# Statistics taken at each update of the residual, slot rows transposed two slots ahead, and bias rows and range test moved: a four-layer gated decoder on one core

## The chip, the cores and the metric

The kernel runs on one core of one Trainium2 chip. The metric is the device time of one execution in microseconds (us). The time before is the median of three runs; the profile is of a further execution. Engines are named as in the profile: PE (TensorE matmul), PEld (its weight loads), DVE (VectorE), ACT (ScalarE), POOL (GpSimd) and SP (SyncE, here a DMA queue).

## What is computed

x is [16, 128, 256] in float32: 16 sequences (b) of 128 rows with 256 features. Eight updates follow each other, each with the layer norm of x as input and a gate tanh(g) as factor:

```
x = x + tanh(g_xattn[0]) * xattn0(ctx, ln(x), ...)      # 16 heads of 16
x = x + tanh(g_ffn[0])   * moe0(ln(x))                  # 8 experts, best 2, hidden 1024, gelu
x = x + tanh(g_xattn[1]) * xattn1(ln(x), ctx, ...)      # softmax over the queries, biases
x = x + tanh(g_ffn[1])   * (ln(x) @ base + b + lora by softmax gates)
x = x + tanh(g_xattn[2]) * xattn2(ctx, ctx, ln(x), mask)
x = x + tanh(g_ffn[2])   * (moe2(ln(x)) + shared expert) # 8 experts, best 2, hidden 512, swiglu
x = x + tanh(g_xattn[3]) * xattn3(ctx, ln(x))           # keys: ctx and x together, 8 heads of 64
x = x + tanh(g_ffn[3])   * moe3(ln(x))                  # 8 experts, best 2, hidden 256, silu

def ln(x): (x - mean) / sqrt(var + 1e-5)
```

## The kernel before

x stays on the chip as 16 tiles `xs[b]` of [128 rows, 256]. They are worked in 4 blocks (`blk`) of 4. A norm of a block (`ln_block`, or `residual` in layer 3) is a chain over three engines: `ln_stats` takes bn_stats and bn_aggr of the four tiles on DVE (lines 242, 243), `inverse_sd` takes Ln and Exp on ACT and a Newton step on DVE (lines 219 to 232), `normalized` makes xn on ACT (257, 261), PE transposes it (284) and ACT copies it back (288).

Attention (`attend`) has its order on PE, ACT and DVE written by hand: everything between runs in program order on these engines. Steps over b make scores, values and output; the output's last operation adds into xs[b] (`add_scaled`, line 320). Between their parts they call `tick()`, which advances each waiting job (a generator) whose count has run out; a job's `yield n` asks for n ticks. Jobs are the preparation of the next block (with `fetch`, which adds an expert layer's output to xs, line 509), and what lies `behind` a block: in layers 0, 2 and 3 `Moe.front`, in layer 1 `Lora.run`. In the last stretch of `attend` (`late`) every yield counts as one tick.

An expert layer sorts its rows. `front` takes the norm, the router's logits (366), softmax and best two, works out a place for each row and scatters the rows to DRAM (`xg`, line 473, eight indirect DMAs on POOL for each block); `plan` says which expert each of 39 slots of 128 rows belongs to. Then slots run: SP loads rows (`xr`, line 689) five slots ahead and weights by expert; PE transposes the rows (722), DVE copies them (`xT`, 724); PE does the two matmul layers (1349, 1525 or 1573, and 759); DVE weighs the output (`y`, 765 or 767); POOL scatters it to DRAM (`yd`, 768) by row numbers `to` (745), which have OUT = 8 buffers. Slots that are surely full start early, beside the attention's last block (layer 0), or beside the last front (layer 3). Of an iteration in `slots` the order is:

```python
first(s + near)
hT = yield from hidden(get, lane(s), xTs.pop(s), lambda *ps: when(s, *ps))
turn(s + 1)
hidden_of.append((s, hT))
if len(hidden_of) > depth:
    finish(*hidden_of.pop(0))
weigh(s + 1)
load(s + far)
second(s + near2)
```

Slots outside `attend` and other operations that stand outside it in the program are ordered by a planner, by its own costs and by what they depend on; it may put them between the operations of `attend`. Two such are of use here. `split_biases` (line 2001 on) makes of four bias rows three bfloat16 parts each, which PE adds by one matmul; three of the rows are read from `rows`, a tile loaded once at the start (line 2070). `Watch.fine` (1014 to 1019) compares sums of range with a bound; POOL collects them (1012). The result of that test decides at the end whether a slower general version runs.

Of the kernel before, what the change touches and what calls it, by code (L numbers as in the profile page):

```python
# [31 lines left out]
NE = 8  # L32
# [29 lines left out]
SURE = 2 * B + 1  # L62
OUT = 8
LANES = 3
# [26 lines left out]
def kernel(ctx: ExitStack, tc: tile.TileContext, a: dict, out: bass.AP):  # L91
# [142 lines left out]

    def ln_stats(srcs, twice=False):


        n = len(srcs)
        mv = stat.tile([P, n, 2], F32, tag="mv", name="mv", bufs=4)
        for i, src in enumerate(srcs):  # L240
            st = stat.tile([P, 6], F32, tag="bnst", name="bnst", bufs=4)
            nc.vector.bn_stats(st, src)
            nc.vector.bn_aggr(mv[:, i, :], st)
            if i % 2 and i < n - 1:
                yield 1
        rstd = yield from inverse_sd(mv[:, :, 1], n, twice)
        return mv, rstd

    def normalize(dst, src, mv, rstd, i):
# [18 lines left out]
    def block(blk):  # L268
        return range(blk * BPB, (blk + 1) * BPB)

    def ln_block(blk, see=None):


        mv, rstd = yield from ln_stats([xs[b] for b in block(blk)])
        if see is not None:
            see(rstd)
        xns = yield from normalized([xs[b] for b in block(blk)], mv, rstd)
        yield 4
        xt = xtpool.tile([P, KC, TB], F32, tag="xnT", name="xnT")
        for pair in range(BPB // 2):  # L280
            ps = ps_x.tile([P, KC, 2 * S], F32, tag="x", name="ps_ln")
            for j in range(2):
                for k in range(KC):
                    nc.tensor.transpose(
                        ps[:, k, j * S:(j + 1) * S],
                        xns[:, pair * 2 + j, k * P:(k + 1) * P], ident,
                    )
            nc.scalar.copy(xt[:, :, pair * 2 * S:(pair + 1) * 2 * S], ps)
            yield 1 if pair == 0 else 3
        return xns, xt  # L290
# [10 lines left out]

    def thirds(tag, bias_row, rest):

        t = rpool.tile([P, D], BF16, tag=tag, name="bias3", bufs=1)
        first, second, third = (slice(i * 32, (i + 1) * 32) for i in range(3))
        nc.vector.tensor_copy(t[0:96], bias_row[0:96])
        nc.vector.tensor_tensor(rest[0:96], bias_row[0:96], t[0:96], ALU.subtract)
        nc.vector.tensor_copy(t[second], rest[second])
        nc.vector.tensor_copy(t[third], rest[third])
        nc.vector.tensor_tensor(rest[third], rest[third], t[third], ALU.subtract)  # L310
        nc.vector.tensor_copy(t[third], rest[third])
        return t
# [19 lines left out]
    def softmax8(lg):  # L332
        m = tiny("sm_m")
        nc.vector.tensor_reduce(m, lg, AX.X, ALU.max)
        d = small("sm_d")
        nc.vector.tensor_tensor(d, lg, bc(m), ALU.subtract)
        e = small("sm_e")
        nc.scalar.activation(e, d, AF.Exp)
        yield 3
        s = tiny("sm_s")  # L340
        nc.vector.tensor_reduce(s, e, AX.X, ALU.add)
        r = tiny("sm_r")
        nc.vector.reciprocal(r, s)
        p = small("sm_p")
        nc.vector.tensor_tensor(p, e, bc(r), ALU.mult)
        return p
# [28 lines left out]
    class Moe:  # L375
# [4 lines left out]
        def __init__(self, layer, wg, turn, see=None):  # L380
            self.layer, self.wg, self.turn, self.see = layer, wg, turn, see
            self.carry = region
            self.done = None
            self.scatters, self.returns = [], []

# [3 lines left out]
        def front(self, blk, plan=None):  # L389

            xns, xnT = yield from ln_block(blk, self.see)
            lg = yield from router_logits(xnT, self.wg, NE)
            soft = softmax8(lg)
            next(soft)
            if self.layer == 2:
                yield 3
                p = finish(soft)
                key = small("key")
                nc.vector.tensor_tensor(
                    key, p, row("gate_b")[:, None, :].to_broadcast([P, BPB, NE]), ALU.add  # L400
                )
            else:
                key = lg
# [94 lines left out]
        def fetch(self, pool, blk):  # L498
# [8 lines left out]
            for i, b in enumerate(block(blk)):  # L507
                for j in range(2):
                    nc.vector.tensor_tensor(xs[b], xs[b], ys[i][:, j], ALU.add)
                yield 1  # L510

# [115 lines left out]
        def slots(self, n, plans, lanes, get, fetch1, fetch2, hidden, nf, far, depth):  # L627
# [126 lines left out]
            def finish(s, hT):  # L754
# [9 lines left out]
                if bias is None:  # L764
                    nc.vector.tensor_scalar(y, po, c[:, 1:2], None, ALU.mult)
                else:
                    nc.vector.scalar_tensor_tensor(y, po, c[:, 1:2], bias, ALU.mult, ALU.add)  # L767
                self.unordered(nc.gpsimd.indirect_dma_start(  # L768
# [14 lines left out]
            yield 1  # L783
            turn(0)
            weigh(0)
            hidden_of = []
            for s in range(n):
# [3 lines left out]
                hT = yield from hidden(get, lane(s), xTs.pop(s), lambda *ps: when(s, *ps))  # L791
                turn(s + 1)
                hidden_of.append((s, hT))
# [209 lines left out]
    class Watch:  # L1003
# [9 lines left out]

        def fine(self, good):

            eq = stat.tile([P, self.n], F32, tag="wz", name="wz", bufs=1)
            nc.vector.tensor_scalar(eq, self.sum, HUGE, None, ALU.is_le)
            nc.vector.tensor_reduce(good, eq, AX.X, ALU.add)
            return self.n * P
# [4 lines left out]
    class Fast16:  # L1024
# [184 lines left out]
        def output(self, b, tick):  # L1209
# [7 lines left out]
            if self.bias is not None:  # L1217
                add_row(py, self.bias)
            add_scaled(b, py, self.gate)
            tick()  # L1220

# [5 lines left out]
    def attend(parts, most=(99, 1), filler=None, open_end=False):  # L1227
# [29 lines left out]
        with tc.manual_schedule(engines=IN_ORDER):  # L1257

            tc.keep_in_program_order(nc.scalar.add_instruction(
                mybir.InstLoadActFuncSet(  # L1260
                    name=nc.get_next_instruction_name(), ins=[], outs=[], act_func_set_id=LN_EXP
                )
            ))
            ready = ahead(*blocks[0][:2], 0)
            for n in range(len(steps) + 2):
# [6 lines left out]
                if n < len(steps):  # L1272
                    if n % BPB == 0:

                        while any(job in jobs for job in ready):
                            tick()
                        if n // BPB + 1 < len(blocks):
                            att, before, _, blk = blocks[n // BPB + 1]
                            ready = ahead(att, before, blk)
                    att, b = steps[n]  # L1280
                    att.scores(b, tick)
# [81 lines left out]
    class Lora:  # L1363
# [10 lines left out]
        def run(self, blk):  # L1374
# [30 lines left out]
            for i, b in enumerate(block(blk)):  # L1405
# [7 lines left out]
                add_row(po, self.bias)  # L1413
                add_scaled(b, po, tgf(1))
                yield 1

# [194 lines left out]
    class Attention3:  # L1611
# [4 lines left out]
        def run(self, blk):  # L1616
# [3 lines left out]
            cts, ys = [], []  # L1620
            mv, rstd = finish(ln_stats([xs[b] for b in block(blk)]))
            for i, b in enumerate(block(blk)):
# [94 lines left out]
    class Fast3:  # L1717
# [106 lines left out]
        def residual(self, blk, before):  # L1824

            yield from before
            xb = [xs[b] for b in block(blk)]
            mv, both = yield from ln_stats(xb, twice=True)
            t = self.pool.tile([P, KC, TB], F32, tag="kvx", name="kvx")
# [124 lines left out]
        def output(self, b, tick):  # L1954
            oT = self.os.pop(b).rearrange("p i c s -> p (i c) s")
            py = ps_x.tile([P, D], F32, tag="x", name="ps_y")
            for k in range(4):
                nc.tensor.matmul(
                    py, lhsT=oT[:, k, :], rhs=self.w[3][:, k, :], start=(k == 0), stop=(k == 3)
                )  # L1960
            add_scaled(b, py, self.gate)
            tick()

# [35 lines left out]
    wgs, biases = {}, {}  # L1999

    def split_biases(t):

        nc.vector.tensor_scalar(row("l2_bo"), row("l2_bo"), 1 / DOWN, None, ALU.mult)
        for i, name in enumerate(("l1_bo", "l2_bo", "base_b")):
            biases[name] = thirds(name, row(name), t[:, 1 + i, 0:D])
        nc.vector.tensor_scalar(row("l2_bo"), row("l2_bo"), DOWN, None, ALU.mult)
        biases["sb"] = thirds("sb3", t[:, 0, 0:D], t[:, 1, 0:D])

    def layers(fast):
        first_turn = 1 if fast else 4  # L2010

# [34 lines left out]
        with tc.tile_pool(name="context", bufs=1) as cpool, ExitStack() as for_mid:  # L2046
# [16 lines left out]
            with tc.tile_pool(name="att0", bufs=2) as pool:  # L2063
# [16 lines left out]
                def clear(blk):  # L2080
                    if blk == 1:
# [9 lines left out]
                        for i in range(0, ROWS, n * P):  # L2091
# [5 lines left out]
                            )  # L2097
                    if blk == 2 and fast:
                        mask.extend(mask_by_keys(cpool, mi))
# [30 lines left out]
            with for_slots, tc.tile_pool(name="lanes0", bufs=2) as pool:  # L2130
                lanes = lanes + lane0(pool, LANES - len(lanes))
                job = slots0(moe, NSLOT - n, plans[-1:], lanes, tiles(fpool, bufs0))
                for i, _ in enumerate(job):
                    if i == 24:
                        ws = [attention_weights(layer, wpool) for layer in (1, 2)]
                        if not biases:

                            t = stat.tile([P, BPB, ROW], F32, tag="xn", name="bias_rows", bufs=3)
                            nc.sync.dma_start(
                                out=t[:, 0, 0:D],  # L2140
                                in_=a["l2_b2"][NE:NE + 1].to_broadcast([P, D]),
                            )
                    if i == 48 and not biases:
# [99 lines left out]
        with tc.tile_pool(name="last", bufs=1) as pool:  # L2243
            moe3.last(pool)

    layers(fast=True)

    watches = (watch, watch1, watch3)
    good = const.tile([P, len(watches)], F32, tag="good", name="good")
    want = sum(w.fine(good[:, i:i + 1]) for i, w in enumerate(watches))  # L2250
    ps = ps_x.tile([1, len(watches)], F32, tag="x", name="ps_good")
# [102 lines left out]
```

## Time and profile before

| | |
|---|---|
| runs | 1712.75 us median (1705.27, 1712.75, 1713.97) |
| profiled execution | 1708.5 us, of which the span is 1706.8 |
| PE busy | 1557.9 us (91%), granted clock 0.96 |
| PEld, DVE, ACT, POOL busy | 1197.2, 892.7, 636.6, 285.2 us |
| DMA | 169.29 MB, mean 99 GB/s |

Stages by the timeline: attention of layer 0 until about 150 us, its slots until 425, layers 1 and 2 (attention and Lora) until 840, layer 2's slots until 1237, attention of layer 3 until 1520, the last slots until 1673, the last additions until 1707. A row of the timeline has start, duration, engine, line, operation, out<-in, and in brackets the idle time before it with what ended it. A row of the waits has who waited for whom, the total in us, the number of times and the longest. "issue" is a wait for nothing that the profile shows.

### The profile page before, as it was taken

To read this page: it belongs to the slowest core of one execution; us is meant where nothing else is said; L and a number is where in the kernel's file an instruction comes from. 1 tells how busy PE (TensorE), PEld (TensorE's weight loads), DVE (VectorE), ACT (ScalarE), POOL (GpSimd) and SP (SyncE) were. 2 spreads that over 40 slices of the span, in tenths; PEclk is the share of its full clock that TensorE was granted. 3 is DMA by queue.
4 is the path that set the end of the run, shared out by engine and by line. 5 is a ranking of instruction groups with operands and counts; after the bars stand their busy time and mean duration, and the time that the engine had idled before them with its cause. 6 is when DMAs were issued, how large, how long until landed. Compare 5 with 4: busy or idle time off the path is not lost. (4 is left out here: it accounts for less than half of the span.)

```text
span 1706.8 us, 34879 instructions
## 1 busy us (share of the span) xinstructions
PE 1557.9 (91%) x12803; PEld 1197.2 (70%) x12803; DVE 892.7 (52%) x2915; ACT 636.6 (37%) x1504; POOL 285.2 (17%) x364
## 2 busy tenths in 40 slices
PE   4998999999889999998999999999989999986891
PEld 2666889999455566664459999999836665666891
DVE  2676521221477655665545555556724645556554
ACT  3554533345444454544224333334443323223010
POOL 4122411111000000221100111111100002114433
PEclk8998999999988999899999999999999999998996
DMA  9505675342200000110054323411220100033855
GB/s 336 216 27 181 202 254 166 116 144 86 87 26 1 1 14 14 39 39 26 26 192 149 132 70 98 153 30 30 94 68 26 38 2 26 20 113 109 271 161 184
DMA packets 110456, 169.29 MB, mean 99 GB/s; under 512 B 16697, under 2 KB 83710, under 8 KB 110272
## 3 DMA queue, kind: packets, MB, share of 16 engines
q1 hardware_dynamic: 92320, 118.28, 22.0%
q0 software_dynamic: 13392, 43.37, 6.8%
q10 hardware_dynamic: 4560, 5.25, 0.9%
q8 instruction: 108, 1.77, 0.4%
q14 instruction: 76, 0.62, 0.1%
HBM read 268.42 MB, written 48.18 MB: 185 GB/s over the span
## 5 line engine op out<-in xcount | busy, mean ns | idle before, releaser
L1525 PE MATMUL ps_w<-xT,w 128*128 128x128 f32 x2304 | 266.4, 275 | 0.0
L1525 PEld LDWEIGHTS ps_w<-xT,w 128*128 128x128 f32 x2304 | 264.0, 192 | 2.1
L768 POOL DMA_INDIRECT yd<-y,to x117 | 118.2, 1011 | 574.2 <-DVE y L767 382.7
L759 PE MATMUL ps_e<-w,hT 128*128 128x256 f32 x848 | 197.8, 380 | 3.0 <-DVE hT L1430 1.3
L759 PEld LDWEIGHTS ps_e<-w,hT 128*128 128x128 f32 x848 | 154.6, 190 | 22.8 <-PE ps_w L678 2.2
L1533 ACT ACTIVATE u<-ps_w,b 128x128 f32<-128x128 f32 x312 | 89.6, 368 | 174.9 <-PE ps_w L1525 169.3
L1536 DVE SCALAR_TENSOR_TENSOR m<-ps_w,b,u 128x128 f32<-128x128 f32 x312 | 87.5, 344 | 104.2 <-PE ps_w L1525 96.0
L1349 PE MATMUL ps_h<-xT,w 128*128 128x128 f32 x1120 | 133.5, 278 | 8.7 <-DMA w<-in_l_w_dram 7.8
L1349 PEld LDWEIGHTS ps_h<-xT,w 128*128 128x128 f32 x1120 | 130.0, 194 | 10.7 <-issue 6.9
L1354 ACT ACTIVATE hT<-ps_h,b 128x128 f32<-128x128 f32 x312 | 89.4, 375 | 115.2 <-issue 82.8
L767 DVE SCALAR_TENSOR_TENSOR y<-ps_e,c,bias 128x256 f32<-128x256 f32 x78 | 37.7, 483 | 180.8 <-PE ps_e L759 179.7
L473 POOL DMA_INDIRECT xg<-xn,xi x96 | 94.6, 985 | 129.9 <-issue 78.0
L1460 PE MATMUL ps_w<-xnT,sw 128*128 128x512 f32 x256 | 111.8, 593 | 0.0
L1012 POOL TENSOR_TENSOR sum_range<-sum_range,rs 128x256 f32<-128x256 f32 x48 | 35.2, 733 | 426.7 <-DVE rs L1203 187.7
L1460 PEld LDWEIGHTS ps_w<-xnT,sw 128*128 128x128 f32 x256 | 47.9, 190 | 57.3 <-issue 50.9
L1137 PE MATMUL ps_s<-qM,kT 32*128 32x256 f32 x768 | 80.4, 444 | 7.3 <-ACT e L1152 6.4
L261 ACT ACTIVATE xn<-x,nmr,rstd 128x256 f32<-128x256 f32 x128 | 67.4, 599 | 30.7 <-DVE nmr L257 30.7
L1203 DVE RECIPROCAL rs<-ps_o 128x256 f32<-128x256 f32 x32 | 56.2, 1756 | 39.9 <-PE ps_o L1192 39.8
L1137 PEld LDWEIGHTS ps_s<-qM,kT 32*128 32x128 f32 x768 | 41.8, 192 | 42.1 <-issue 21.1
L1152 ACT ACTIVATE e<-ps_s 128x512 f32<-128x512 f32 x128 | 65.7, 600 | 12.0 <-PE ps_s L1137 12.0
L1573 PE MATMUL ps_g<-xT,kT 128*128 128x128 f32 x296 | 44.4, 296 | 24.4 <-DVE xT L724 11.5
L751 ACT ACTIVATE bias<-b,c 128x256 f32<-128x256 f32 x78 | 40.3, 517 | 64.1 <-DMA b<-in_l_b_dram 25.2
(278 smaller groups left out, 2582.2 us busy)
## 6 DMA issues: line engine op xcount, KB each, us to landing
w<-in_l_w_dram SPq DMA_DIRECT2D x156, 1024.0 KB
w<-in_l_w_dram SPq DMA_DIRECT2D x39, 512.0 KB
kT<-in_l_wgu_dram SPq DMA_DIRECT2D x39, 512.0 KB
xg<-zeros POOLq DMA_DIRECT2D x15, 1170.0 KB, 25.6
yr<-yd SPq DMA_DIRECT2D x40, 256.0 KB
xr<-xg SPq DMA_DIRECT2D x78, 130.0 KB
b<-in_l_b_dram SPq DMA_DIRECT2D x78, 128.0 KB
kT<-in_l_w_dram SPq DMA_DIRECT2D x39, 256.0 KB
```

The source lines that it names most:

```text
L261: nc.scalar.activation(xns[:, i, 0:D], src, AF.Identity, bias=nmr[:, i:i + 1], scale=rstd[:, i:i + 1])
L473: self.unordered(nc.gpsimd.indirect_dma_start(out=xg[:, :], in_=xns[:, i, :], in_offset=None, out_offset=bass.IndirectOffsetOnAxis(ap=xi[: ...
L759: nc.tensor.matmul(po, lhsT=hT[:, f, :], rhs=lane(s)["w2"][:, f, :], start=(f == 0), stop=(f == nf - 1),)
L768: self.unordered(nc.gpsimd.indirect_dma_start(out=yd[:, :], in_=y, in_offset=None, out_offset=bass.IndirectOffsetOnAxis(ap=to[:, 0:1], axi ...
L1137: nc.tensor.matmul(pss[j][:, 2 * c:2 * c + 2, :], lhsT=self.kT[blk][part, c, tok], rhs=self.qM[blk][part, c, :, tok], start=True, stop=True,)
L1152: nc.scalar.activation(e, pss[j], AF.Exp)
L1349: nc.tensor.matmul(ps[:, i, :], lhsT=w["w1"][:, k, f * P:(f + 1) * P], rhs=xT[:, k, :], start=(k == 0), stop=(k == KC - 1),)
L1354: nc.scalar.activation(hT[:, f, :], ps[:, i, :], AF.Gelu, bias=w["b1"][:, f:f + 1])
L1460: nc.tensor.matmul(ps, lhsT=wt[:, k, f * P:(f + 1) * P], rhs=xnT[:, k, :], start=(k == 0), stop=(k == KC - 1),)
L1525: nc.tensor.matmul(ps[:, f, :], lhsT=wt[:, k, s, f * P:(f + 1) * P], rhs=xT[:, k, :], start=(k == 0), stop=(k == KC - 1),)
L1533: nc.scalar.activation(u[:, f, :], pair[0][:, f, :], AF.Identity, bias=w["b1"][:, i:i + 1])
L1536: nc.vector.scalar_tensor_tensor(m1[:, f, :], pair[1][:, f, :], w["b3"][:, i:i + 1], u[:, f, :], ALU.add, ALU.mult,)
```

## The change

Eight edits, none of which alters what is computed:

1. `ready(b)` takes the statistics of xs[b] (bn_stats, bn_aggr) right behind each update of it: behind `add_scaled` in the outputs of attention, in Lora, and behind the additions of `fetch`. The norms take them from `seen`; only layer 0's first norm still computes them itself. A norm has one `yield` less.
2. In `slots`, `turn(s + 2)` in place of `turn(s + 1)`, with `turn(1)` at the start.
3. OUT is 16 in place of 8.
4. `split_biases` reads four rows that are loaded for it in the middle of layer 0's slots, none from `rows`.
5. `fine` is tied behind the `y` of slot 33 of layer 3, in another buffer.
6. The front of the last block of an expert layer loads the table set that holds Ln and Exp by an instruction of its own.
7. `softmax8` yields once between the subtraction of the maximum and Exp.
8. The mask of layer 2 is made before block 3 of layer 0 in place of block 2.

```diff
-OUT = 8
+OUT = 16
...
-    def ln_stats(srcs, twice=False):
...
+    def ready(b):
+
+        blk, i = divmod(b, BPB)
+        if run["fast"]:
+            if i == 0:
+                seen[blk] = new_mv()
+            mean_var(seen[blk], i, xs[b])
...
+    def ln_residual(blk, twice=False, own_set=False):
+
+        mv = seen.pop(blk, None)
+        if mv is None:
+            mv = new_mv()
+            for i, b in enumerate(block(blk)):
+                mean_var(mv, i, xs[b])
+        if own_set:
+            ln_exp()
+        rstd = yield from inverse_sd(mv[:, :, 1], BPB, twice)
+        return mv, rstd
...
         nc.vector.tensor_tensor(d, lg, bc(m), ALU.subtract)
+        yield 1
         e = small("sm_e")
         nc.scalar.activation(e, d, AF.Exp)
-        yield 3
+        yield 2
...
+            own_set = run["fast"] and blk == NBLK - 1
+            xns, xnT = yield from ln_block(blk, self.see, own_set)
...
                 for j in range(2):
                     nc.vector.tensor_tensor(xs[b], xs[b], ys[i][:, j], ALU.add)
+                ready(b)
                 yield 1
...
             turn(0)
+            turn(1)
             weigh(0)
...
-                turn(s + 1)
+                turn(s + 2)
...
-            eq = stat.tile([P, self.n], F32, tag="wz", name="wz", bufs=1)
-            nc.vector.tensor_scalar(eq, self.sum, HUGE, None, ALU.is_le)
+            eq = rpool.tile([P, D], F32, tag="gbias", name="in_range", bufs=1)[:, :self.n]
+            tc.add_manual_dep(
+                nc.vector.tensor_scalar(eq, self.sum, HUGE, None, ALU.is_le).ins, behind.name,
...
             add_scaled(b, py, self.gate)
+            ready(b)
             tick()
...
+    on_pe = [
+        (name, a["rows"][:, slice(*_ROWS[name])]) for name in ("l1_bo", "l2_bo", "base_b")
+    ] + [("sb", a["l2_b2"][NE:NE + 1])]
+
     def split_biases(t):
-
-        nc.vector.tensor_scalar(row("l2_bo"), row("l2_bo"), 1 / DOWN, None, ALU.mult)
-        for i, name in enumerate(("l1_bo", "l2_bo", "base_b")):
-            biases[name] = thirds(name, row(name), t[:, 1 + i, 0:D])
-        nc.vector.tensor_scalar(row("l2_bo"), row("l2_bo"), DOWN, None, ALU.mult)
-        biases["sb"] = thirds("sb3", t[:, 0, 0:D], t[:, 1, 0:D])
+        for k, (name, _) in enumerate(on_pe):
+            v = t[:, k, 0:D]
+            if name == "l2_bo":
+                nc.vector.tensor_scalar(v, v, 1 / DOWN, None, ALU.mult)
+            biases[name] = thirds("three_" + name, v)
...
-                    if blk == 2 and fast:
+                    if blk == NBLK - 1 and fast:
                         mask.extend(mask_by_keys(cpool, mi))
...
+        return moe3.weighted[NSLOT - 6]
```

## The prediction

> **What bounds the kernel now.** I read the page first, then the gaps of PE in the waits of that engine, then the timeline around each long gap.
>
> ```profile
> span 1706.8 us, 34879 instructions
> PE 1557.9 (91%) x12803; PEld 1197.2 (70%) x12803; DVE 892.7 (52%) x2915; ACT 636.6 (37%) x1504; POOL 285.2 (17%) x364
> PE ps_ln L284 <- ACT xn L261: 16.1, 5, 11.4
> PE ps_g L1573 <- DVE xT L724: 11.5, 3, 4.0
> PE ps_g L1573 <- issue: 9.7, 6, 2.8
> ```
>
> PE is busy 91% of the span, so only its gaps (1706.8 - 1557.9 = 149 us) and its slow clock can be won. 33.7 us of the gaps are the end, after the last matmul at 1673 (scatters, reload, last additions), which the change leaves alone. The two largest other groups are a wait of 11.4 us for xn, and the waits of the layer 3 slots (L1573) for xT. The timeline of the start tells the first:
>
> ```profile
> 11.95 0.71 DVE L229 SCALAR_TENSOR_TENSOR nt<-r,ve 128x4 f32<-128x4 f32 x1 [1.49 <-ACT r L226]
> 22.33 0.29 DVE L2003 TENSOR_SCALAR rows<-rows 128x256 f32<-128x256 f32 x1 [9.67 <-DMA rows<-in_rows_dram]
> 22.54 0.15 DVE L230 TENSOR_TENSOR nt<-nt,r 128x4 f32<-128x4 f32 x1
> 23.28 2.08 ACT L261 ACTIVATE xn<-x,nmr,rstd 128x256 f32<-128x256 f32 x4 [10.06 <-DVE nmr L257]
> ```
>
> DVE is in the middle of the first norm when it meets L2003, the scaling inside split_biases, and stands 9.67 us until the rows have landed; the rest of the norm is queued behind. ACT and PE wait for it. The timeline of layer 3, where the last front runs between the first 12 slots:
>
> ```profile
> 1534.64 0.41 DVE L724 COPY xT<-ps_xr 128x256 f32<-128x256 f32 x1
> 1535.16 2.05 PE L1573 MATMUL ps_g<-xT,kT 128*128 128x128 f32 x8 [2.77 <-issue]
> 1549.62 0.17 DVE L1017 TENSOR_SCALAR wz<-sum_range 128x4 f32<-128x4 f32 x1 [5.18 <-POOL sum_range L1012]
> 1550.89 0.41 DVE L724 COPY xT<-ps_xr 128x256 f32<-128x256 f32 x1
> 1573.13 1.13 PE L1573 MATMUL ps_g<-xT,kT 128*128 128x128 f32 x8 [2.52 <-issue]
> 1588.89 0.15 DVE L745 TENSOR_SCALAR to<-c 128x1 int32<-128x1 f32 x1 [3.97 <-DMA yd<-y,to]
> 1590.44 2.05 PE L1573 MATMUL ps_g<-xT,kT 128*128 128x128 f32 x8 [3.87 <-DVE xT L724]
> ```
>
> Each slot starts when DVE has copied xT, and DVE copies it late: behind a dozen small operations of the front (1534.64), behind the range test, which waits 5.18 us for a POOL that is issuing eight scatters (1549.62), and behind a row number whose buffer a scatter still reads (1588.89). From 1597 on slots follow each other without gaps: PE is busy 73.4 of 75 us. So what is won before 1597 moves the end.
>
> **The change, part by part** (against the profiled execution: span 1706.8, its time 1708.5 us).
>
> *Bias rows split late.* split_biases no longer reads `rows`; its input is loaded at yield 24 of the layer 0 slots, so nothing of it can run at the start. L229 ends at 12.66; L230, L232 and L257 follow at 0.2 us each (as at 36.68, 36.88, 37.07 in block 1), so xn starts at about 13.5 instead of 23.28: -9.8. What is late next: x of block 1 is issued at 6.9 to 9.2, before the rows (10.33), and is now wanted at 32.46 - 9.8 = 22.7, when even the rows had landed. Ends: -11.4 (the whole gap) and -4 (a later load takes half). The 25 operations of the four splits (0.28 a cast, 0.42 a subtraction, some 8 us) ran at 174 to 181 and 308, where PE is busy 48 and 50 of 50 us; between the slots near 300 DVE is busy 10 of 50, so they stay hidden. Three more row loads (128 KB each) cost SP 0.35 us each there, with DMA at 0.3 to 0.5: nothing. If that cover were gone: 8 us.
>
> *Range test behind the slots.* Its operations leave 1518 to 1520 and 1549. The gap of 3.61 before the slot at 1551.36 goes. In the gap of 4.03 before the slot at 1520.08, the test stands from 1518.07 to 1519.44: 1.4. In its new place it takes 0.29 + 0.42 + 2 x (0.17 + 0.17), 1.4 us, on a DVE that is busy 42 of 75, and the sums are complete by then: nothing.
>
> *Sixteen row numbers.* `to` of slot n now waits for the scatter of slot n-16, not n-8. The gap of 3.87 goes. Next in line is y, with 8 buffers, but it is made three slots later, so its scatters have landed.
>
> *Rows transposed two slots ahead.* PE's order keeps the same transposes, DVE's the same copies, but slot s+1 no longer starts on a copy made in the same turn. The gaps that end on a late xT: 2.77 + 2.57 + 2.46 + 2.52 + 0.64 = 10.96. DVE is busy 15.3 of 22 us from 1550 to 1572 and PE 16.4, so the front's operations must still fit beside the slots. Ends: nothing and 10.96; I take half, 5.5, since neither engine is full.
>
> *The clock.* Behind the gaps of 2.77, 3.61 and 3.87 the eight ps_g matmuls took 2.05 to 2.08 us, behind 2.46, 2.52 and 2.57 they took 1.13. Measured on the rows that follow: 1.5, 1.8 and 2.9 us (the last with transposes and ps_e). These go with their gaps.
> [...]
>
> Layer 3 slots: 3.6 + 1.8 + 1.4 (test), 3.9 + 2.9 (row numbers), 5.5 + 1.5 (xT): -20.6; ends -7 (row numbers alone) and -30.3 (all gaps from 1516 on with their clock).
>
> *Statistics behind each update.* 112 pairs (28 blocks of 4; the 16 of layer 0's start stay) of 0.40 + 0.18 us move from the front of a norm to behind the add. The sum of DVE is unchanged. It shortens a chain where PE waits on it: at the start of layer 3 the last add ends at 1260.04, the four pairs end at 1263.77, xn frees PE only at 1265.92 after a gap of 3.96. With three pairs done earlier the chain is 2.5 shorter. In the start of layer 1 the gap of 2.53 ends on ACT's Ln behind ten kT copies, so nothing. Elsewhere queued on DVE behind the pair stand the v copy, the sums or the reciprocal of the next step: 0 taken, ends -6 and +6, a fifth of the 32 us of PE gaps that stand between 440 and 840, all ended by DVE or ACT. Each norm loses one tick, each front of layers 0 and 3 gets it back between d and exp, so slots and front keep their order.
>
> *Own table set, exp one tick later, mask one block later.* Three fronts get one explicit load for two (1283 ns each: 167.52 and 170.14, for example). ACT is busy 37%, so 0; ends -3.8 and 0. The mask's gap of 1.70 at 54 moves with it: 0.
> [...]
>
> *What it adds.* In the first slots job of layer 0 the second row block must arrive before the first hidden matmul:
>
> ```profile
> 146.46 0.38 SPq L1302 DMA_DIRECT2D w<-in_l_w_dram  x1
> 148.40 0.38 SPq L1302 DMA_DIRECT2D w<-in_l_w_dram  x1
> 149.29 2.47 SPq L689 DMA_DIRECT2D xr<-xg  x2
> 151.70 0.55 PE L1349 MATMUL ps_h<-xT,w 128*128 128x128 f32 x1 [3.86 <-DMA w<-in_l_w_dram]
> ```
>
> PE starts at 151.70, 5.2 after the issue of w1. xr of slot 1 is issued behind w2 (148.40, 1 MB), so by the same 5 to 7 us it lands near 155.5; PE stands, with the rest of layer 0's attention queued behind: +4.0; ends 0 and +8. The other jobs load earlier, or wait for w1 of slot 1 anyway (237.94).
>
> Sum: -9.8 - 20.6 - 2.5 + 4.0 = -28.9, so 1708.5 becomes 1679.6. The profiled execution is 4.2 below the median of the three runs (1712.75), from which the same sum gives 1683.9. I take **1682**, the sum from halfway (1710.6).
>
> **Rivals.**
> *The front keeps DVE.* If the front's chain (ACT and DVE by turns, one step a tick) sets the pace from 1530 to 1586, the xT gaps come back as other gaps, and only the row numbers stay won: -7 instead of -20.6, so -15.3: about 1695. For it: DVE has 15.3 of 22 us. Against: the test's 5.18 us is plain waiting.
> *A later load swallows the start.* DMA is at 0.96 until 50 us, with 15 zero fills of 1.2 MB. At -4 instead of -9.8: about 1688. Against: the tiles wanted next were issued before the rows.
> *Waits only move.* Both happen and layers 1 and 2 lose 6: -15.3 + 5.8 + 6 = -3.5, about 1707: no change. A change of 0.5% (8.6 us) is about what a measurement of this kernel can tell.
> *Slower: the pairs lie bare.* Place: DVE in attention of layers 1 to 3, busy 28 to 39 of 50, between an output's add and the next reciprocal. Price 0.59 for each of 112, at most 66 us. It decides once 37.5 us (28.9 + 8.6), 64 of the 112, are bare; with 75 bare (44 us) the time is about 1726. Against: the same pairs are in DVE's queue already, and PE waited on one only for 2.7 us in all.
>
> **How the numbers follow.** Forecast 0.58; front keeps DVE 0.20; start swallowed 0.06; waits only move 0.09; slower 0.07. Faster by over 0.5% is 0.58 + 0.20 + 0.06 = 0.84, same 0.09, slower 0.07. The range goes down to 1668 (start whole, layer 3 two thirds of the way to its end, table sets at theirs, no cost in layer 0: -9.8 - 27.1 - 2.5 - 3.8 = -43.2) and up to 1706, which takes in the first two rivals and part of the third: about 0.2 lie outside.
>
> **What would show it.** Right: no DVE wait for rows, first ps_ln near 14; L1017 after 1620; no L745 wait for yd; ps_g gaps under 1.5 us from 1530 to 1590; slot 0 of layer 0 later after its w1 than now. Wrong: a PE gap of over 5 us near 14 to 30 on a load; ps_g gaps ended by ACT sg or by DVE hT instead; more PE idle in 440 to 840 than the 32 us of now.

## The result, and the profile after

The changed kernel takes 1688.12 us (median of 4 runs, 1680.81 to 1688.69), the kernel before beside it 1713.36 us. The ratio is 0.9853, 95% interval [0.9812, 0.9893]: faster by 1.5%. The forecast was 1682 with a range of 1668 to 1706. The profiled execution took 1688.69 us, its span is 1686.9.

The page of the changed kernel:

```profile
span 1686.9 us, 34935 instructions
...
PE 1553.8 (92%) x12803; PEld 1202.8 (71%) x12803; DVE 900.5 (53%) x2914; ACT 631.5 (37%) x1501; POOL 285.1 (17%) x364
```

The waits of PE (who waited for whom, us in total, times, longest):

```profile
PE ps_ln L321 <- ACT xn L298: 12.4, 8, 4.3
PE ps_xr L766 <- DMA xr<-xg: 11.3, 2, 10.7
PE ps_kv L1809 <- ACT xn L298: 10.4, 4, 3.9
...
PE ps_g L1624 <- DVE xT L768: 3.3, 1, 3.3
```

and of layer 3's `ps_kv` before:

```profile
PE ps_kv L1758 <- ACT xn L261: 7.1, 3, 4.0
```

The wait of 11.4 us for the first xn is gone, and the waits of the layer 3 slots for xT fell from 11.5 to 3.3. Two others are new: one of 10.7 us for `xr`, and a fourth wait of layer 3's `ps_kv` for xn (10.4 us in all, 7.1 before). Split at five places that both traces have, the span's end among them (us):

| | before | after | difference | forecast |
|---|---|---|---|---|
| layer 0 (attention, slots) | 423.1 | 424.0 | +0.9 | -5.8 |
| layers 1 and 2, to the second block of layer 2's slots | 438.4 | 423.7 | -14.7 | 0 |
| rest of layer 2's slots | 360.6 | 360.7 | +0.1 | 0 |
| attention of layer 3 | 288.8 | 296.5 | +7.7 | -2.5 |
| last slots and end | 195.9 | 182.0 | -13.9 | -20.6 |
| span | 1706.8 | 1686.9 | -19.9 | -28.9 |

So the total came out nearly as forecast, but out of other parts. The timeline of the start shows the first step as forecast:

```profile
11.29 0.16 DVE L229 SCALAR_TENSOR_TENSOR nt<-r,ve 128x4 f32<-128x4 f32 x1 [0.90 <-ACT r L226]
11.49 0.16 DVE L230 TENSOR_TENSOR nt<-nt,r 128x4 f32<-128x4 f32 x1
...
13.10 2.07 ACT L298 ACTIVATE xn<-x,nmr,rstd 128x256 f32<-128x256 f32 x4
13.85 2.07 PE L321 MATMUL ps_ln<-ident,xn 128*128 128x128 f32 x8 [1.26 <-ACT xn L298]
```

L229 and L230 follow each other at 0.2 us, with no wait for rows between them, and xn starts at 13.10 in place of 23.28. At 140 us the changed kernel is still 9.1 ahead by its additions to xs. The timeline of 139 to 153, rows of PE and SP alone, shows where that goes:

```profile
139.84 0.38 SPq L1352 DMA_DIRECT2D w<-in_l_w_dram  x1
...
141.78 0.38 SPq L1352 DMA_DIRECT2D w<-in_l_w_dram  x1
142.67 4.46 SPq L733 DMA_DIRECT2D xr<-xg  x4
...
152.06 0.66 PE L766 MATMUL ps_xr<-ident,xr 128*128 128x128 f32 x2 [10.68 <-DMA xr<-xg]
...
152.51 0.85 PE L1399 MATMUL ps_h<-xT,w 128*128 128x128 f32 x3
```

The first expert matmul starts 12.7 us after the issue of w1 (139.84); before it was 5.2 (146.46 to 151.70). The row block of slot 1, issued at 142.67 behind w2, lands 9.4 later, and PE stands 10.68 for it, in `turn(1)`. From the issue of w1 that is 7.4 more than before; w1 itself was issued 6.6 earlier. At 170 us the lead is gone. In the last front, PE's rows in the timeline are:

```profile
1515.56 2.00 PE L1624 MATMUL ps_g<-xT,kT 128*128 128x128 f32 x8 [3.33 <-DVE xT L768]
...
1527.73 1.06 PE L1624 MATMUL ps_g<-xT,kT 128*128 128x128 f32 x8
...
1531.31 1.13 PE L1624 MATMUL ps_g<-xT,kT 128*128 128x128 f32 x8 [0.55 <-issue]
...
1538.72 0.93 PE L321 MATMUL ps_ln<-ident,xn 128*128 128x128 f32 x4 [4.30 <-ACT xn L298]
```

Slots follow each other (0.55), but the front's own transposes now wait 4.30 for xn, and its rank 2.40 for `both`, from 1554.75 on: part of the gaps only changed owner. Layers 1 and 2, and the attention of layer 3, by windows (PE, PEld, DVE, ACT, POOL busy, then PE's granted clock); first before, then after:

```profile
423.00:861.00 438.00, 406.02 (x3140) 245.88 (x3139) 261.96 (x750) 191.19 (x344) 54.98 (x72) 0.94 0.08 27
...
1222.00:1511.00 289.00, 275.53 (x2624) 175.19 (x2623) 149.08 (x405) 96.19 (x199) 30.64 (x37) 0.99 0.12 38
```

```profile
424.00:848.00 424.00, 395.70 (x3142) 241.83 (x3141) 265.52 (x751) 189.75 (x343) 54.78 (x72) 0.96 0.09 28
...
1208.00:1505.00 297.00, 281.04 (x2562) 177.10 (x2561) 148.66 (x406) 96.06 (x200) 30.49 (x37) 0.97 0.11 35
```

Both differences are the clock more than the gaps. The traces have the clock at half speed (granted share 0.50) in stretches of 3.41 us or a multiple, but for the last, which ends with the trace; eight ps_g matmuls took 2.00 us in one of them (1515.56, after) and 1.06 outside (1527.73). Layers 1 and 2 have 51.2 us of them before and 34.1 after: 17.1 us at half speed less is an estimated 8.5 us of work, and the gaps fell by 3.7 (32.0 to 28.3): 12.2 of the 14.7. In layer 3's attention it is the other way round: 6.8 us at half speed before, 20.5 after (an estimated 6.9 of work; PE's busy time grew by 5.5), and gaps of 13.5 and 16.0 (2.5).

### The profile page after: what moved, and what is told of

Read it like the earlier page. It is cut to its first block, busy times and chain, and to the rows that moved or that the text cites. A ratio compares the mean times of both kernels' runs of the same rounds, so it can differ in the third digit from the quotient of the medians.

```text
span 1686.9 us, 34935 instructions
## 1 busy us (share of the span) xinstructions
PE 1553.8 (92%) x12803; PEld 1202.8 (71%) x12803; DVE 900.5 (53%) x2914; ACT 631.5 (37%) x1501; POOL 285.1 (17%) x364
## 4 chain that ended last, share of the span: by engine, by line
PE 77%; DVE 11%; DMA 5%; ACT 4%; issue 1%; SPq 0%; POOL 0%; ACTq 0%; DVEq 0%
PE ps_w L1576 15%; PE ps_e L803 12%; PE ps_h L1399 7%; PE ps_w L1511 6%; PE ps_qk L1833 5%; PE ps_o L1246 3%; PE ps_v L1942 3%; PE ps_s L1191 2%; PE ps_g L1624 2%; PE ps_k L912 2%; PE ps_q L912 2%; PE ps_o L1980 2%; PE ps_s L1533 2%; PE ps_u L1624 2%; DVE rs L1257 2%; PE ps_router L405 2%
## 5 line engine op out<-in xcount | busy, mean ns | idle before, releaser
L768 DVE COPY xT<-ps_xr 128x256 f32<-128x256 f32 x117 | 48.4, 416 | 66.1 <-PE ps_xr L766 66.1
L1191 PE MATMUL ps_s<-qM,kT 32*128 32x256 f32 x768 | 72.3, 429 | 4.9 <-ACT e L1206 4.9
L1191 PEld LDWEIGHTS ps_s<-qM,kT 32*128 32x128 f32 x768 | 41.2, 192 | 34.1 <-issue 17.9
```

The costliest lines, as they stand in the source:

```text
L1191: nc.tensor.matmul(pss[j][:, 2 * c:2 * c + 2, :], lhsT=self.kT[blk][part, c, tok], rhs=self.qM[blk][part, c, :, tok], start=True, stop=True,)
```

## Experiments

The variants ran on two chips on which the kernel before takes 1758 to 1762 us, not 1713 (the chip of the first comparison is not on record); ratios are to the kernel before on the same chip (the second chip had test_and_numbers_undone, exp_tick_undone, one_tick_no_exp_tick and two_ticks). The stages of their profiled executions, in us, split as above (layer 2's slots, 360.5 to 360.8 in all, are left out). Up to layer 3's last front, test_and_numbers is the kernel before, and stands for it; in the last slots rows_late_alone is the kernel before.

A row's stages are those of one execution, its ratio is of medians. Executions of one kernel differ by 3 to 17 us (two_ahead_alone: 1749.1 to 1758.3, and its trace is of one of 1757.4), so the sum of a row's stages need not follow its ratio:

| | layer 0 | layers 1, 2 | layer 3 attention | last slots, end | ratio |
|---|---|---|---|---|---|
| test_and_numbers | 437.2 | 446.9 | 309.0 | 200.2 | 1.0003 [0.9985, 1.0020] |
| rows_late_alone | 435.1 | 448.5 | 309.2 | 201.2 | 0.9950 [0.9919, 0.9981] |
| two_ahead_alone | 447.6 | 449.7 | 309.1 | 188.5 | 0.9928 [0.9897, 0.9959] |
| the changed kernel | 437.2 | 440.4 | 307.0 | 186.8 | 0.9847 [0.9815, 0.9880] |
| turn1_behind | 430.5 | 438.7 | 309.6 | 189.0 | 0.9836 [0.9792, 0.9881] |
| test_and_numbers_undone | 436.5 | 436.0 | 307.1 | 189.2 | 0.9822 [0.9799, 0.9844] |
| exp_tick_undone | 441.4 | 439.4 | 310.7 | 187.1 | 0.9829 [0.9807, 0.9852] |
| statistics_in_norm | 437.8 | 446.1 | 298.5 | 181.3 | 0.9826 [0.9794, 0.9858] |
| tick_back | 444.8 | 426.4 | 295.6 | 180.4 | 0.9689 [0.9647, 0.9731] |
| tick_and_turn | 432.5 | 427.0 | 294.6 | 184.9 | 0.9694 [0.9662, 0.9726] |
| one_tick_no_exp_tick | 439.9 | 427.0 | 309.3 | 185.3 | 0.9774 [0.9754, 0.9794] |
| two_ticks | 431.1 | 419.1 | 296.5 | 187.7 | 0.9657 [0.9637, 0.9677] |

**The changed kernel itself**, so that the others stand beside it.

> The changed kernel as it is, so that it stands beside the variants on one chip. Theory: the early transpose costs 5 to 9 us that turn1_behind (ratio 0.9836) saved, so the ratio is 0.986 to 0.989, with the gap of about 10 us before the transposes of slot 1 in layer 0. Rival (the early transpose costs nothing in the end, since the weights of slot 1 come no sooner): the ratio is 0.983 to 0.985.

0.9847, the gain of the first comparison, and the rival's number, though the interval reaches into the theory's range (0.986 to 0.989): on the whole time the early transpose is not resolved. The parts differ from the first comparison: layers 1 and 2 gain 6.5 here, not 14.7, and layer 3's attention gains 2.0 where it lost 7.7. Part of that is chance in the clock: the three traces here that are the kernel before in layers 1 and 2 (test_and_numbers, two_ahead_alone, rows_late_alone) have 47.8, 58.0 and 61.4 us at half clock there; the changed kernel has 58.0.

**The start and the early transpose.** First the bias rows alone, in the kernel before:

```diff
     def split_biases(t):
...
-            biases[name] = thirds(name, row(name), t[:, 1 + i, 0:D])
...
+        for k, (name, _) in enumerate(on_pe):
+            v = t[:, k, 0:D]
...
+            biases[name] = thirds("three_" + name, v)
```

> Kernel before with the bias rows alone loaded and split late. Theory: the DVE wait of 9.67 us for rows is gone, the first ps_ln starts near 14 instead of 24, and since slot 1 is transposed where it was, all of it reaches the end: 9 to 10 us faster (about 1703 against 1713). Rival (layer 0's slots are paced by weight transfers): the lead at 140 us is 9 us but at 440 us under 3, and the time is within 4 us of the kernel before.

The third block's first output (`ps_y`) in layer 0 comes at 97.6 us in place of 106.9: -9.3, the size forecast. In the trace 7.1 of that are left at the first expert matmul and 2.1 at the end of layer 0, as the rival had it; but the ratio of 0.995 is 8.8 us, with an interval of 3 to 14, as the theory had it. So how much of a gain at the start reaches the end is not settled.

Then the transpose of slot 1 behind the first hidden half, in the changed kernel:

```diff
             turn(0)
-            turn(1)
...
+                if s == 0:
+                    turn(1)
                 turn(s + 2)
```

> Changed kernel, but the rows of slot 1 are transposed behind the first hidden layer instead of ahead of it. Theory (the second transpose waits for rows that land behind two weight transfers, and everything queued on PE behind it waits too): PE's gap of 10.68 us at 141 shrinks to the wait for w1, 3 to 4 us; the 9.3 us that layer 0's attention had gained by then stay, and the time is about 9 us less than the changed kernel's 1688 (1679). Rival (slots of layer 0 are paced by the weight transfers, so an earlier start only waits at the next weights): the gap splits into later waits for w near 200 to 240, and the time stays within 3 us of 1688.

The gap of 10 us on `xr` is gone (the first expert matmul starts 5.5 us after w1, at 154.68 and 149.19), and layer 0 is 6.7 shorter. In tick_back and tick_and_turn, which differ by this edit alone, layer 0 is 12.3 shorter, and two slots ahead alone make it 10.4 longer (two_ahead_alone against test_and_numbers). By the first issue of w1 the kernels of these pairs are already 2 to 5 us apart. From that issue the first expert matmul comes 12.6 to 13.5 us later in every trace with the early transpose, 5.0 to 5.6 in every one without: the price is 7 to 8.5 us, not 4. Whether the end keeps it is open: the intervals of 0.9836 and 0.9847 overlap, and so do those of 0.9694 and 0.9689 of the other pair.

**Two slots ahead alone**, in the kernel before:

```diff
             turn(0)
+            turn(1)
...
-                turn(s + 1)
+                turn(s + 2)
```

> Kernel before with the rows transposed two slots ahead alone. Theory: PE's wait in the first slots of layer 0 grows from 3.9 to 8 to 11 us (loss of 4 to 7), and of the 11 us of gaps on a late xT in layer 3, 5 to 11 go; together -5 to +2 us against 1713. Rival (the front's chain, not xT, paced those slots): layer 3 keeps its gaps under other names, gains under 3 us, and the kernel is 3 to 6 us slower.

The last slots are 11.7 shorter than in test_and_numbers and 12.7 shorter than in rows_late_alone, layer 0 is 10.4 longer. The ratio of 0.9928 is 12.7 us (interval 7 to 18), more than the -5 to +2 expected and than this trace's stages add up to.

**Range test and row numbers**, alone in the kernel before (OUT = 16, and the test tied behind slot 33), and taken back in the changed kernel:

> The kernel before with two edits of the change alone: the range test behind the slots, and 16 row numbers. Up to layer 3's last front it is the kernel before. Theory: the gaps of PE that ended on the late range test (3.6 and 1.4 us) and on the row number whose buffer a scatter still read (3.9 us) go with their slow clock (4.7 us): 13.6 us, ratio 0.992. Rival (the front sets the pace): only the row numbers stay won, 7 us, ratio 0.996. Rival (gaps come back elsewhere in the front): 0.999 to 1.000.

> The changed kernel with two edits taken back: the range test stands again beside the last front of layer 3, and there are 8 row numbers. PE, ACT, POOL and SP have the same instructions in the same order as in the changed kernel; DVE has the six operations of the test earlier. Theory of the prediction (the test and the row numbers cost 13.6 us where they stood): 1740 to 1748 where the changed kernel has 1734 on this chip, ratio 0.990 to 0.993, with a DVE wait of 3 to 5 us for sum_range and one of 3 to 4 us for yd. Rival (rows transposed two slots ahead had already taken the DVE copy out of the way of PE, so that the test and the row numbers wait beside a busy PE): ratio 0.984 to 0.986, as the changed kernel, with the same DVE waits but no PE gap behind them.

```diff
-OUT = 16
+OUT = 8
...
-            eq = rpool.tile([P, D], F32, tag="gbias", name="in_range", bufs=1)[:, :self.n]
-            tc.add_manual_dep(
...
-                reason="not in the way of the slots",
-            )
...
+            eq = stat.tile([P, self.n], F32, tag="wz", name="wz", bufs=1)
+            nc.vector.tensor_scalar(eq, self.sum, HUGE, None, ALU.is_le)
```

Alone they bring nothing that shows (1.0003, the last rival's number; last slots 200.2 against 201.2 in rows_late_alone). On this chip another wait holds DVE at the same place. The timeline of test_and_numbers, POOL, DVE and ACT:

```profile
1588.97 0.97 POOL L473 DMA_INDIRECT xg<-xn,xi  x1 [0.30 <-issue]
1590.25 1.00 POOL L771 DMA_INDIRECT yd<-y,to  x1 [0.30 <-issue]
1591.25 0.24 POOL L1015 TENSOR_TENSOR sum_range<-sum_range,rstd 128x4 f32<-128x4 f32 x1
1592.07 0.42 DVE L1589 TENSOR_TENSOR hT<-ps_u,sg 128x256 f32<-128x256 f32 x1 [5.74 <-remote]
...
1592.85 0.59 ACT L288 COPY xnT<-ps_ln 128x512 f32<-128x512 f32 x1 [3.70 <-remote]
```

No test stands there any more, and DVE still waits 5.74 until POOL's scatters are issued, for something that no event of the program ends ("remote"). So this run cannot tell what the test cost on the chip of the first comparison, where no such wait is found. The other direction can be read: in test_and_numbers_undone the wait of the test is back, and its timeline shows PE beside it:

```profile
1575.96 2.43 PE L321 MATMUL ps_ln<-ident,xn 128*128 128x128 f32 x8 [4.31 <-ACT xn L298]
...
1578.19 3.57 PE L405 MATMUL ps_router<-wgl,xnT 128*128 128x8 f32 x16
...
1581.61 2.06 PE L1624 MATMUL ps_g<-xT,kT 128*128 128x128 f32 x8
1581.68 0.17 DVE L1071 TENSOR_SCALAR wz<-sum_range 128x4 f32<-128x4 f32 x1 [5.61 <-issue]
```

DVE stands 5.61 us, and PE works through: xT of the next slot had been copied a turn earlier. No DVE wait for `yd` came back. The last slots are 2.4 longer than in the changed kernel; the ratio shows no loss. With the rows two ahead, the rival holds: test and row numbers are worth 2.4 us at most in these traces, not 13.6.

**The statistics and the ticks.** The norm yields once where its statistics are taken already:

```diff
             for i, b in enumerate(block(blk)):
                 mean_var(mv, i, xs[b])
+        else:
+            yield 1
```

> Changed kernel with the one yield put back at the head of each norm whose statistics are already there; the statistics stay at the updates. Theory (the missing tick moves PE's transposes nearer to the update, which cost layer 3's attention 9 us and happened to fit layers 1 and 2 better by 15 us): layer 3's attention gets back 6 to 9 us, layers 1 and 2 lose 10 to 15 us, together 2 to 8 us slower than 1688. Rival (the place of the statistics on DVE does both): both stretches stay as in the changed kernel within 3 us, and so does the time.

0.9689 where the changed kernel has 0.9847, against both the theory (slower) and its rival (no change): the yield that the change leaves out is worth 1.6%. Layers 1 and 2 are 14.0 shorter, layer 3's attention 11.4, the last slots 6.4; layer 0 is 7.6 longer. In layers 1 and 2 PE's gaps are much the same (32.4 and 30.5 us), and the time at half clock falls from 58.0 to 27.3, an estimated 15.4 us of work. In the four traces with early statistics and this tick it is 27 to 34 us, in the other eight from these chips 44 to 61. Which gaps the half clock stood behind there was not followed. In layer 3's attention the waits of `ps_kv` for xn fall from 10.4 to 5.8 us, gaps that nothing explains from 4.4 to 2.5, and time at half clock from 27.3 to 17.1 (an estimated 5.1 of work). One such wait is seen in the timeline of the changed kernel (of the first comparison), and then of tick_back:

```profile
1409.31 0.16 DVE L294 SCALAR_TENSOR_TENSOR nmr<-mv,rstd 128x4 f32<-128x4 f32 x1
...
1412.27 0.16 DVE L219 TENSOR_SCALAR ve<-mv 128x4 f32<-128x4 f32 x1
1412.46 0.20 ACT L224 ACTIVATE lv<-ve 128x4 f32<-128x4 f32 x1 [9.73 <-DVE ve L219]
...
1412.81 1.07 ACT L298 ACTIVATE xn<-ct,nmr,rstd 128x256 f32<-128x256 f32 x2
...
1413.45 1.18 PE L1809 MATMUL ps_kv<-ident,xn 128*128 128x128 f32 x4 [3.87 <-ACT xn L298]
```

```profile
1429.00 0.16 DVE L296 SCALAR_TENSOR_TENSOR nmr<-mv,rstd 128x4 f32<-128x4 f32 x1
...
1429.20 1.09 ACT L300 ACTIVATE xn<-ct,nmr,rstd 128x256 f32<-128x256 f32 x2 [6.79 <-DVE nmr L296]
...
1430.41 0.66 PE L1811 MATMUL ps_kv<-ident,xn 128*128 128x128 f32 x4
...
1432.15 0.21 ACT L224 ACTIVATE lv<-ve 128x4 f32<-128x4 f32 x1 [0.89 <-DVE ve L219]
```

Two norms overlap in layer 3, that of the context (`ct`) and that of x. Without the tick the Ln of x's norm (L224) stands on ACT ahead of xn of the context. Its `ve` is made on DVE only behind the front's positions, so xn, ready at 1409.5, starts at 1412.81, and PE waits 3.87. With the tick, xn goes first, as soon as nmr is there.

> The changed kernel with the statistics again taken in the front of the norm, with the yield between the second and the third pair as before; all the other edits stay. Theory (it is the tick that moves the fronts, and the place of the 112 pairs is worth little): within 0.4% of the tick alone, ratio 0.967 to 0.973; layer 3's attention without the three gaps of 2.4 to 3.9 us on xn around 1330 to 1415. Rival (the place of the pairs brought the 15 us that layers 1 and 2 gained): layers 1 and 2 lose those 15 us again, ratio 0.976 to 0.980. Rival (neither): as the changed kernel, 0.985.

```diff
-        if run["fast"]:
+        if False:
...
                 mean_var(mv, i, xs[b])
+                if i == 1:
+                    yield 1
```

0.9826, against the theory, and between its two rivals (0.976 to 0.980, and 0.985); the stages speak for the first, that the place of the pairs counts. The statistics in their old place, tick kept, cost layers 1 and 2 what they gain with tick_back (446.1 against 426.4; the kernel before 446.9), and layer 3's attention little (298.5 against 295.6). So the early statistics are worth 1.4% with the tick. The edit as it was made, early statistics and one tick less, brings nothing that these runs resolve (0.9847 against 0.9826); early statistics against late ones with the tick left out in both were not run.

> The changed kernel without the yield between the subtraction of the maximum and Exp; the wait behind Exp is one tick longer again. Theory (the place of the norm in PE's order is what costs, and softmax comes behind it): within 0.3% of the changed kernel, ratio 0.982 to 0.988. Rival (this tick takes ACT's table load and Exp off a path on which PE waits): slower by the waits on Exp, ratio 0.990 or more.

```diff
         nc.vector.tensor_tensor(d, lg, bc(m), ALU.subtract)
-        yield 1
...
-        yield 2
+        yield 3
```

0.9829, as the changed kernel and as the theory had it: alone this tick brings nothing that these runs resolve.

**Both mends, and more.** tick_back and turn1_behind together; the same without the tick ahead of Exp; the same with `yield 2` in the norm:

> The changed kernel with two edits taken back in part: a norm that finds its statistics taken yields once in their place (as in tick_back), and the rows of slot 1 are transposed only behind the first hidden half of slot 0 (as in turn1_behind). Theory (the missing tick costs in layers 1 to 3, and the early transpose costs in layer 0; the two lie in different stages): both gains add. Layer 0's first hidden matmul again follows its w1 by the same time as before, with no gap of over 5 us on xr, some 6 to 13 us earlier than with the tick alone; ratio about 0.961 to 0.965 where the tick alone had 0.969. Rival (the wait in layer 0 only turns into the next wait for weights): ratio 0.969, as with the tick alone. Rival (the tick alone was a good placement by chance and shifts with any other edit): 0.975 or more, with other gaps of PE in layer 3's attention.

> As tick_and_turn, but without the yield between the subtraction of the maximum and Exp. Fronts then have as many ticks as before the change, and PE's transposes of xn stand where they stood before the change. Theory (what brings 1.4% is that the statistics are done earlier while the transposes keep their place): as tick_and_turn, ratio 0.966 to 0.972. Rival (it is the total length of the front that has to fit the slots): 0.975 or more, with the loss in the last front of layer 3.

> As tick_and_turn (a norm that finds its statistics taken yields once; the rows of slot 1 of the first job are transposed behind the first hidden half), but the norm yields twice. PE's transposes of xn then stand one step later once more. Theory (one tick is what the chain over DVE and ACT needs before PE meets the transposes; a second only delays the front and the slots behind it): slower than with one tick, ratio 0.970 to 0.980. Rival (the chain is still late, as the gaps of 2.8 and 3.5 us on xn at the start of layer 3 and in its last front show): those gaps go and the ratio is 0.963 to 0.967.

tick_and_turn is at 0.9694: layer 0 gains the 12.3 of the theory against tick_back, but the whole time is the rival's, as with the tick alone. Without the tick ahead of Exp it is 0.9774, the rival's number, and the loss is not in the last front: it is 14.7 in layer 3's attention and 7.4 in layer 0. On these chips layer 3's attention is short (295 to 299) only in the four traces with both ticks, that is with one more than before the change, and 307 to 311 in all others. Part of that may belong to these chips: in the same four traces DVE and ACT have at most one of the stops told of in the last section in that stage, in the others two or three, and PE's gaps that nothing in the profile explains are 8.6 us in one_tick_no_exp_tick, 1.4 in tick_and_turn. In the first comparison, without such stops, the stage took 288.8 with as many ticks as one_tick_no_exp_tick has. In layers 1 and 2 the tick ahead of Exp does nothing (427.0 in both). A second tick in the norm brings layers 1 and 2 to 419.1; its ratio 0.9657 is the best of all (1697.32 us beside 1758.42), by less than the intervals against one tick. Against the expectation it did not cost more than it brought, and it did not remove the waits of layer 3's `ps_kv` for xn (6.5 us against 6.9), as the rival had it do.

## Why the prediction was right, and where it was not

- *Total and direction*: right, in the range, and by luck so near: -25.2 by the medians where -28.9 was forecast, out of errors that cancel. Three stages were forecast too good (layer 0 by 6.7, the last slots by 6.7, layer 3's attention by 10.2), and layers 1 and 2 gained 14.7 that were not forecast. On the chip that had them all, the edits tried alone give 0.9950 (bias rows), 0.9928 (two slots ahead) and 1.0003 (test and numbers), together 0.988 beside 0.9847 for all eight; the difference is within the intervals.
- *Bias rows, -9.8*: right for the start (first ps_ln at 13.85, -9.1 at 140 us; -9.3 alone). Its sign of failure, a gap of over 5 us at 14 to 30, looked in the wrong place: of the gain, 6.6 were left when w1 was issued at 139.84, and the wait for `xr` took them.
- *The wait added in layer 0, +4.0*: the mechanism was right, the size not: 7.4 in the trace, 7 to 8.5 in the pairs. I had let `xr` land 5 to 7 us after its issue, an estimate from w1's 5.2; behind w2 of 1 MB it took 9.4.
- *Layer 3 slots, -20.6*: -13.9. The sum gave each gap to one cause and added the causes. On the other chips two_ahead_alone already brings 11.7; test and row numbers add 2.4 to that, not 13.6: in test_and_numbers_undone DVE stands 5.61 us and PE works on, its xT made a turn earlier. "The front keeps DVE" was half right: 4.30 on xn and 2.40 on `both` are the front's chain. The profile signs held: the test runs at 1646.50, no DVE wait for `yd`, and of the ps_g gaps from 1530 to 1590 one alone is over 1.5 (1.65, on weights).
- *Statistics, 0 in layers 1 and 2 and -2.5 in layer 3*: wrong in both. The wait that was priced did shrink, from 3.96 to 2.07 us; the step that failed is "Each norm loses one tick, each front of layers 0 and 3 gets it back between d and exp, so slots and front keep their order." The norm stands ahead of d, so without its tick it moves against the steps of attention around it; tick_back shows what that costs, 1.6% on its chip.
- *The clock*: I priced it behind the gaps of the last slots alone. It carries most of what happened in layers 1 and 2 (an estimated 8.5 of the 14.7; forecast 0) and in layer 3's attention (an estimated 6.9, PE's busy time 5.5, where the stage lost 7.7; forecast -2.5).
- *Slower, by bare pairs*: not seen. DVE's busy time in layers 1 and 2 is 262.0 before and 265.5 after, and the gaps there fell.

What stays open: what the tick and the single edits are worth on the chip of the first comparison, why the clock stays up longer in layers 1 and 2 with early statistics and the tick, and whether the time that the later transpose saves in layer 0 reaches the end.

## What to carry to other kernels

When an edit takes an instruction out of a hand-made order, ask first what the count of steps still orders: the work that was made earlier may be worth less than the place that the rest had. When several causes hold up the same slots, price them together (the whole gap once), not one gap for each cause. Price a wait of PE with the clock behind it, in every stage; and follow a gain at the start to the next wait for a transfer before it is put into the sum.

## What the runs showed of the hardware

*Half clock came in stretches of 3.41 us and multiples of it.* Of the 21 stretches at half clock before, 12 were 3.41 us long, 6 were 6.83, and one each 10.24, 17.07 and 30.71, the last up to the trace's end; of the 20 after, 11 were 3.41, 6 were 6.83, and one each 10.24, 13.65 and 33.40, the last again up to the trace's end. In each of these two traces all changes of the clock lie on one grid of 3.413 us, to within 4 ns. After a PE gap of 1.62 us (from 759.08, after) a stretch began at 761.32; after one of 2.07 (from 1239.30, before) none did before 1265.09, and after one of 2.08 at the same step (from 1225.56, after) one began at 1228.95. So in these three cases the length of the gap alone does not tell whether half clock follows.

*On two chips DVE and ACT stood while POOL issued scatters.* The twelve traces from there have 101 stops of DVE or ACT of over 3 us that end on "remote", 38 to 84 us in each trace. All of them end within 2.1 us of the end of an indirect scatter on POOL; a third of the span lies as near to one. The two traces of the first comparison have none. There ACT copies at the same step with no wait, between the same scatters (timeline of before):

```profile
1547.08 0.97 POOL L473 DMA_INDIRECT xg<-xn,xi  x1 [0.30 <-issue]
1547.15 1.21 ACT L288 COPY xnT<-ps_ln 128x512 f32<-128x512 f32 x2
1548.35 1.00 POOL L768 DMA_INDIRECT yd<-y,to  x1 [0.31 <-issue]
```

With them go gaps of PE over 0.3 us that nothing explains: 20 to 45 us in each trace from the two chips, 10.4 and 1.9 in the two of the first comparison. What the engines wait for there was not tried.
